# Two expert layers written in their own order, with the gate of a convolution layer and parts of an attention layer spread over other work

## The chip, the cores and the metric

The kernel runs on one core of one Trainium2 chip. The metric is the device time of one execution in microseconds (us), as the median of several runs. One further execution was recorded by the hardware profiler; durations of single instructions come from it.

A core has five engines that run at the same time, each through its own list of instructions in order: TensorE (PE in the profile) for matrix products, which writes to PSUM; VectorE (DVE), ScalarE (ACT) and GpSimd (POOL) for elementwise work; and SyncE (SP), which here only issues transfers (DMAs). PSUM has eight banks of 512 float32 columns on 128 partitions. An instruction that needs another engine's result waits on a semaphore, and everything behind it on its engine waits too.

## The reference

The input is `x` of shape (4, 128, 64, 64): four images of 128 channels and 4096 pixels. Four layers follow, all in float32.

```python
x = x + conv0(group_norm(x))                  # layer 0: deformable convolution
x = g * x + x                                 # layer 1, with
#   o = batch_norm(mamba_branch(x)); g = sigmoid(conv4_w^T o + conv4_b)
t = tokens(x)                                 # (4, 4096, 128)
t = t + attn2(layer_norm(t))                  # layer 2: cosines, products, a 2048-wide FFN of 8 inputs
t = t + moe2(layer_norm(t))                   #          eight experts, two used
t = t + attn3(layer_norm(t))                  # layer 3: additive tanh attention, causal
t = t + moe3(layer_norm(t))                   #          eight experts, two used
out = t back as (4, 128, 64, 64)
```

An expert layer computes, for each token `v` (128 values after the layer norm):

```python
p = softmax(v @ router_w + router_b)                  # 8 experts
top_p, top_i = top_k(p, 2); top_p = top_p / sum(top_p)
y = sum(top_p[k] * (v @ expert_w[top_i[k]] + expert_b[top_i[k]]) for k in 0, 1)
```

Attention of layer 3 is `w = tril(exp(w2 . tanh(f_i + g_j + b1) + b2))`, rows divided by their sums, times `v`.

## The kernel before, in words

The whole activation stays in SBUF as `X`, 128 partitions by 16384 columns. Through layers 0 and 1 partitions are channels; after that `X` holds tokens on partitions, as 128 tiles `T[:, t, :]` of 128 tokens by 128 channels. The stages run one after the other: layer 0, layer 1, the gate of layer 1, layer 2's attention and FFN, the first expert layer, attention of layer 3, the second expert layer, and a last transpose to channels (`flip`).

Where a stage uses `InOrder`, its instructions stand on each engine in the order in which the Python code writes them (they carry the line number 82 in the profile). Elsewhere a scheduler puts them in an order of its own, by what it expects to be ready.

**The gate (end of `layer1`).** The branch's output `o` lies in DRAM as 32 pieces `kept[k]` of 128 by 512. For each piece: a DMA reads it (`oin`), PE multiplies by `conv4_w` (`psg`), ACT takes the sigmoid (`g`), DVE computes `X = (g + 1) * X`. Two pieces later PE turns the piece's four 128 by 128 blocks to tokens (`psf`), and ACT (even pieces) or DVE (odd pieces) copies them back into `X`. All of it comes before layer 2.

**Layer 2 (`layer2`).** Sixteen groups of eight token tiles go through `slot(p, s)`: 17 + 3 passes `p` from -3 on, eight slots each. In a pass the FFN of group `p` runs on PE (`phh` hidden products, `pff` output products, 1024 of the latter in all), while group `p + 3` gets its moments and norm (`stA`, `u`, `c`), group `p + 2` its cosines and running products (`a`) and second norm, group `p - 1` its last norm and sum. The passes -3 to -1 prepare the first groups and have no FFN: a ramp.

**An expert layer (`moe`).** It is not in written order. It loads router and expert matrices on ACT's DMA queue, subtracts their last row from all others (so that the constant 1 in the last channel of `v` can carry the bias), and works in eight groups of 16 tiles. `route(g)`: moments on DVE (`bn_stats`), norm on ACT (`v`), 16 transposes on PE and copies on ACT (`vT`), 16 products of 8 columns for the logits with tokens on partitions (`psl`), then softmax and the two best experts in some 28 small DVE operations (`gate`). `experts(...)`: per tile two products of 512 columns (`pex`, 128 tokens by 8 experts by 128 channels, three buffers of two banks), one DVE multiplication by the gates over all 1024 columns (`x`), and then the sum over experts: for three tiles of four as three halving additions on POOL and a fourth that adds to `T`, for the fourth tile as one DVE reduction (`y`) and one POOL addition. `route(g + 1)` is written ahead of `experts(g)`.

**Attention (`attention`).** In written order, in 544 steps: 17 per block of 512 queries on average, `4 * ib + 3` for block `ib`. A step has products for a denominator (`D`) and, one step later, a numerator (`num`) on PE, logarithm and exponential on ACT (`r`), multiplications by `num` on DVE, two additions on POOL, and later the weighing (`acc`). `prepare` of the next block is cut into 8 parts (statistics, norm `v`, transposes and copy `vT`, four maps `F`, `G`, an end), spread evenly over a block's steps. After a block's last step `settle` transposes the sums, copies them (`zs`), divides and adds four tiles to `T`, all within one step. `D` has four banks; a step takes three of them, from bank 0 or 1 on (`side`). A part or a `settle` that needs bank 3 makes the step `taken`:

```python
taken = held[-1] is not None or any(p in ON_BANK for p in parts)
side = int(last[0] == 0 and not taken and not last[1])
again = side == last[0]
```

Where `again` holds, the same banks are used as in the step before, and PE begins with the numerator's products in place of the denominator's. The stage ends with a branch on a flag that all engines read.

**`flip`.** 32 rounds after the second expert layer: four transposes on PE (`psf`), a copy by DVE or ACT (`o`), a DMA of 256 KB to the output.

Of the kernel before, what the change touches and what calls it, by code (L numbers as in the profile page):

```python
# [88 lines left out]
class Kernel:  # L89
# [819 lines left out]
    def layer1(self):  # L909
# [9 lines left out]
        GS = NT // NG  # L919
        with ExitStack() as ctx:  # L920
# [4 lines left out]
            dram = ctx.enter_context(tc.tile_pool(name="l1d", bufs=1, space=DRAM))  # L925
# [8 lines left out]
            conv4_w = self.load(cp, "conv4_w", [P, P])  # L934
# [472 lines left out]
            sb = sp.tile([P, 1], F32, name="sb")  # L1407
# [9 lines left out]
            nc = InOrder(tc)  # L1417

            def gate(k):
                ks = slice(k * 512, (k + 1) * 512)  # L1420
                o = gp.tile([P, 512], F32, name="oin", tag="tm", bufs=4)
                plain.sync.dma_start(o, kept[k])
                ps = mm("psg")
                nc.tensor.matmul(ps, conv4_w, o, start=True, stop=True)
                g = gp.tile([P, 512], F32, name="g", tag="yT")
                nc.scalar.activation(g, ps, AF.Sigmoid, bias=sb)
                nc.vector.scalar_tensor_tensor(X[:, ks], g, 1.0, X[:, ks], ALU.add, ALU.mult)

            def to_tokens(k):
                ps = mm("psf")  # L1430
                for v in range(4):
                    c = k * 512 + v * P
                    nc.tensor.transpose(ps[:, v * P:(v + 1) * P], X[:, c:c + P], self.ident)
                dst = X[:, k * 512:(k + 1) * 512]
                if k % 2:
                    nc.vector.tensor_copy(dst, ps)
                else:
                    nc.scalar.copy(dst, ps)

            for k in range(NB * NG + 2):  # L1440
                if k < NB * NG:
                    gate(k)
                if k >= 2:
                    to_tokens(k - 2)

    def flip(self):

        tc, nc, X = self.tc, self.nc, self.X
        with ExitStack() as ctx:
            sp = ctx.enter_context(tc.tile_pool(name="flip", bufs=3))  # L1450
            pp = ctx.enter_context(tc.tile_pool(name="flipp", bufs=4, space=PSUM))
            for k in range(NB * 8):
                ps = pp.tile([P, 512], F32, name="psf")
                for v in range(4):
                    c = k * 512 + v * P
                    nc.tensor.transpose(ps[:, v * P:(v + 1) * P], X[:, c:c + P], self.ident)  # L1456
                o = sp.tile([P, 512], F32, name="o")
                if k % 2:
                    nc.vector.tensor_copy(o, ps)  # L1459
                else:  # L1460
                    nc.scalar.copy(o, ps)  # L1461
                nc.sync.dma_start(self.out[k // 8][:, (k % 8) * 512:(k % 8 + 1) * 512], o)
# [50 lines left out]
    def layer2(self):  # L1513
# [8 lines left out]
        with ExitStack() as ctx:  # L1522
# [25 lines left out]
            nc = InOrder(tc)  # L1548
# [5 lines left out]
            def stream(g):  # L1554
                return T[:, g * GT:(g + 1) * GT, :]

# [170 lines left out]

            ON_VECTOR = ((0, 1, 3), (1,), (1,), (1, 3), (1,), (1,), (1, 3), (1,))
# [52 lines left out]

            for p in range(-3, NG + 1):
                for s in range(8):
                    slot(p, s)

    def moe(self, layer):


        tc, nc = self.tc, self.nc
        GT = 16
        T = self.X.rearrange("p (t c) -> p t c", c=P)
        LAST = P - 1
        with ExitStack() as ctx:
            cp = ctx.enter_context(tc.tile_pool(name=f"m{layer}c", bufs=1))
            sm = ctx.enter_context(tc.tile_pool(name=f"m{layer}s", bufs=2))
            vp = ctx.enter_context(tc.tile_pool(name=f"m{layer}v", bufs=2))
# [4 lines left out]

            rw = self.load(cp, f"router_w{layer}", [P, NE])
            ew = self.load(cp, f"expert_w{layer}", [P, NE * P])
            last = cp.tile([P, P], F32, name="last")
            nc.vector.tensor_copy(last, self.ident[:, LAST:P].to_broadcast([P, P]))
            ps = pe.tile([P, NE, P], F32, name="psl_", tag="pex")
            psf = ps.rearrange("p e c -> p (e c)")
            for h in range(2):  # L1810
                nc.tensor.matmul(psf[:, 512 * h:512 * (h + 1)], last, ew[:, 512 * h:512 * (h + 1)],  # L1811
                                 start=True, stop=True)
            nc.vector.tensor_sub(ew, ew, psf)
            ps = pe.tile([P, NE, P], F32, name="psr_", tag="pex")
            nc.tensor.matmul(ps[:, 0, 0:NE], last, rw, start=True, stop=True)
            nc.vector.tensor_sub(rw, rw, ps[:, 0, 0:NE])
            nc.scalar.dma_start(ew[LAST:P, :], self.ins[f"expert_b{layer}"].rearrange("e c -> (e c)").unsqueeze(0))
            nc.scalar.dma_start(rw[LAST:P, :], self.ins["rows"][ROW[f"router_b{layer}"]].unsqueeze(0))
            vs = [cp.tile([P, GT, P], F32, name=f"v{i}") for i in range(2)]
            for v in vs:  # L1820
                nc.gpsimd.memset(v[:, :, LAST:P], 1.0)

# [5 lines left out]
            sh = [P, GT, NE]  # L1828

            def across(x):  # L1830
                return x.unsqueeze(2).to_broadcast(sh)

            def route(g):
                t = T[:, g * GT:(g + 1) * GT, :]
                v = vs[g % 2]
                mean, rstd = self.ln_stats(sm, t, GT)
                nmr = sm.tile([P, GT], F32, name="nmr")
                nc.vector.scalar_tensor_tensor(nmr, mean, -1.0, rstd, ALU.mult, ALU.mult)
                for k in range(GT):
                    nc.scalar.activation(v[:, k, 0:LAST], t[:, k, 0:LAST], AF.Identity,  # L1840
                                         bias=nmr[:, k:k + 1], scale=rstd[:, k:k + 1])
                vT = vp.tile([P, GT, P], F32, name="vT")
                for h in range(GT // 4):
                    ps = pv.tile([P, 512], F32, name="psv")
                    for k in range(4):
                        nc.tensor.transpose(ps[:, k * P:(k + 1) * P], v[:, 4 * h + k, :], self.ident)  # L1846
                    nc.scalar.copy(vT[:, 4 * h:4 * h + 4, :].rearrange("p t c -> p (t c)"), ps)
                psl = pl.tile(sh, F32, name="psl")
                for k in range(GT):
                    nc.tensor.matmul(psl[:, k, :], vT[:, k, :], rw, start=True, stop=True)  # L1850

                pr = sm.tile(sh, F32, name="pr")
                m = sm.tile([P, GT], F32, name="m")
                nc.vector.tensor_reduce(m, psl, AX.X, ALU.max)
                nc.vector.tensor_tensor(pr, psl, across(m), ALU.subtract)
                nc.scalar.activation(pr, pr, AF.Exp)
                nc.vector.tensor_reduce(m, pr, AX.X, ALU.add)
                nc.vector.reciprocal(m, m)
                nc.vector.tensor_tensor(pr, pr, across(m), ALU.mult)

                gate = sm.tile(sh, F32, name="gate")
                one = sm.tile(sh, F32, name="one")
                mx = sm.tile([P, 2, GT], F32, name="mx")
                rk = sm.tile([P, GT], F32, name="rk")
                for k in range(2):
                    nc.vector.tensor_reduce(mx[:, k, :], pr, AX.X, ALU.max)
                    nc.vector.tensor_tensor(one, pr, across(mx[:, k, :]), ALU.is_equal)
                    nc.vector.tensor_tensor(one, one, rank.unsqueeze(1).to_broadcast(sh), ALU.mult)
                    nc.vector.tensor_reduce(rk, one, AX.X, ALU.max)
                    nc.vector.tensor_tensor(one, one, across(rk), ALU.is_equal)  # L1870
                    if k == 0:
                        nc.vector.scalar_tensor_tensor(pr, one, -2.0, pr, ALU.mult, ALU.add)
                        nc.vector.tensor_tensor(gate, one, across(mx[:, 0, :]), ALU.mult)
                    else:
                        nc.vector.tensor_tensor(one, one, across(mx[:, 1, :]), ALU.mult)
                        nc.vector.tensor_add(gate, gate, one)
                nc.vector.tensor_add(m, mx[:, 0, :], mx[:, 1, :])
                nc.vector.reciprocal(m, m)
                nc.vector.tensor_tensor(gate, gate, across(m), ALU.mult)
                return g, vT, gate  # L1880

            def experts(g, vT, gate):
                for k in range(GT):
                    tk = T[:, g * GT + k, :]
# [4 lines left out]
                    x = xp.tile([P, NE, P], F32, name="x", bufs=4)  # L1889
                    nc.vector.tensor_tensor(x, pex, gate[:, k, :].unsqueeze(2).to_broadcast([P, NE, P]), ALU.mult)  # L1890
                    if k % 4 == 3:
                        y = xp.tile([P, P], F32, name="y")
                        nc.vector.tensor_reduce(y, x.rearrange("p e c -> p c e"), AX.X, ALU.add)  # L1893
                        nc.gpsimd.tensor_tensor(tk, tk, y, ALU.add)  # L1894
# [6 lines left out]
            for g in range(1, NB * NT // GT):  # L1901
                ahead = route(g)
                experts(*held)
                held = ahead
            experts(*held)

# [588 lines left out]
```

## Time and profile before

| | us |
|---|---|
| median of 3 runs | 5567.05 (5563.71 to 5577.1) |
| the profiled execution's own time | 5584.88 |
| its span, first to last instruction | 5583.2 |
| gate of layer 1 | about 1938 to 1985 |
| ramp of layer 2, until PE is full | about 1985 to 2049 |
| layer 2, PE full | 2049 to 2691 |
| first expert layer: start, first `x`, end | 2710, 2746.7, about 3058 |
| attention | about 3055 to 5201 |
| second expert layer: start, first `x`, last POOL addition | 5207, 5241.5, 5554.5 |
| last output transfer issued | 5579 |

Stages are read off the first and last start of the tiles named above. In the profile a group is one kind of instruction; "busy" is the time in which the engine ran it, "mean" the duration of one, and the part behind the bar is the time in which the engine stood idle just before, with the engine and tile that ended it. A float32 product of 512 columns shows as two records.

### The profile page before, as it was taken

What the parts mean: (1) busy time and instruction counts of PE and PEld (TensorE: products, weight loads), DVE (VectorE), ACT (ScalarE), POOL (GpSimd) and SP (SyncE); (2) the same over time, 40 slices, a digit from 0 to 9 for tenths busy, and PEclk for the clock granted to TensorE, in tenths of its full rate; (3) what the DMA queues carried; (4) which work ended last, traced back from release to release, by engine and by line L of the source; (5) the groups of instructions that cost most, each with busy time, mean ns of one, the idle gap of its engine ahead of it and who ended that gap; (6) DMA issues with size and microseconds to landing.
All of it is one profiled execution on the core that took longest, in us unless ns stands there. A gap on an engine that the chain in (4) does not pass through costs nothing. (4 is left out here: it accounts for less than half of the span.)

```text
span 5583.2 us, 62833 instructions
## 1 busy us (share of the span) xinstructions
PE 4990.0 (89%) x21718; PEld 2405.5 (43%) x21718; DVE 4020.2 (72%) x7854; ACT 3113.5 (56%) x3785; POOL 3102.9 (56%) x3027
## 2 busy tenths in 40 slices
PE   5898999879999859999887899989998998999887
PEld 3454444436666523333443344434443444444443
DVE  6888898758875577886697665666566666665796
ACT  1221222146654445555421789878988997889431
POOL 0625355414443334543498567666766776667597
PEclk8999999989988779999899899999999999999899
DMA  5545455300000110000000000000000000000001
GB/s 173 133 124 127 127 143 129 83 6 5 12 16 16 41 44 1 1 1 1 6 31 31 1 1 1 1 1 1 1 1 1 1 1 1 1 1 1 5 1 61
DMA packets 66743, 185.21 MB, mean 33 GB/s; under 512 B 13158, under 2 KB 16038, under 8 KB 64744
## 3 DMA queue, kind: packets, MB, share of 16 engines
q1 hardware_dynamic: 55792, 163.68, 9.9%
q0 software_dynamic: 6272, 12.86, 1.4%
q10 hardware_dynamic: 4344, 4.50, 0.3%
q8 instruction: 175, 2.87, 0.2%
q14 instruction: 160, 1.31, 0.1%
HBM read 131.63 MB, written 49.36 MB: 32 GB/s over the span
## 5 line engine op out<-in xcount | busy, mean ns | idle before, releaser
L82 POOL TENSOR_TENSOR r<-r 128x512 f32<-128x512 f32 (+1 forms) x1088 | 1348.7, 1241 | 666.1 <-DVE r L82 610.3
L82 DVE TENSOR_TENSOR r<-r,num 128x1024 f32<-128x1024 f32 (+1 forms) x1088 | 969.9, 926 | 565.0 <-PE num L82 518.1
L82 PE MATMUL D<-F,G 32*128 32x512 f32 (+3 forms) x4608 | 1223.1, 591 | 1.9 <-POOL G L82 1.0
L82 PE MATMUL num<-F,G 32*128 32x512 f32 (+3 forms) x4608 | 1090.1, 606 | 105.0 <-DVE r L82 101.0
L82 ACT ACTIVATE r<-r 128x2048 f32<-128x2048 f32 (+4 forms) x610 | 1018.4, 1679 | 49.2 <-POOL r L82 3.4
L82 ACT ACTIVATE r<-D 128x1536 f32<-128x1536 f32 (+1 forms) x544 | 764.2, 1405 | 210.4 <-PE D L82 178.2
L82 PE MATMUL acc<-pr,ident 128*128 128x512 f32 x1600 | 736.2, 609 | 63.2 <-DVE pr L82 63.0
L82 PEld LDWEIGHTS D<-F,G 32*128 32x128 f32 x4608 | 505.3, 190 | 326.0 <-issue 216.3
L82 PE MATMUL acc<-r,v 128*128 128x512 f32 (+3 forms) x1152 | 608.1, 615 | 2.9 <-DVE aT L82 2.9
L82 PEld LDWEIGHTS num<-F,G 32*128 32x128 f32 x4608 | 394.8, 187 | 414.0 <-DVE r L82 236.1
L1887 PE MATMUL pex<-w_expert_w,vT 128*128 128x512 f32 x1024 | 490.8, 619 | 77.6 <-DVE x L1890 77.5
L1897 POOL TENSOR_TENSOR x<-x 128x512 f32<-128x512 f32 (+2 forms) x576 | 472.3, 820 | 103.5 <-DVE x L1890 73.4
L82 POOL DMA_INDIRECT px<-tab,idx x196 | 359.4, 1834 | 295.1 <-DVE idx L82 158.5
L82 PEld LDWEIGHTS acc<-pr,ident 128*128 128x128 f32 x1600 | 303.7, 195 | 414.1 <-issue 330.3
L82 DVE TENSOR_TENSOR pr<-v,wt 128x2560 f32<-128x2560 f32 x160 | 453.9, 2843 | 30.7 <-PE acc L82 23.6
L82 PE MATMUL pff<-hid,w_ffn_w2T 128*128 128x512 f32 x1024 | 468.9, 601 | 0.0
L1890 DVE TENSOR_TENSOR x<-pex,gate 128x1024 f32<-128x1024 f32 x256 | 309.0, 1213 | 61.5 <-POOL X L1898 49.9
L82 PEld LDWEIGHTS acc<-r,v 128*128 128x128 f32 x1152 | 177.6, 191 | 395.8 <-issue 266.3
L1887 PEld LDWEIGHTS pex<-w_expert_w,vT 128*128 128x128 f32 x1024 | 184.8, 194 | 328.0 <-DVE x L1890 174.2
L82 ACT ACTIVATE hid<-phh,cols 128x512 f32<-128x512 f32 x320 | 198.9, 685 | 224.7 <-PE phh L82 224.7
L82 POOL TENSOR_TENSOR Y<-y,tm 128x64 f32<-128x64 f32 x256 | 115.4, 471 | 331.9 <-DVE w L82 159.9
L82 POOL TENSOR_TENSOR X<-X,sl 128x512 f32<-128x512 f32 x32 | 90.1, 2817 | 376.1 <-ACT sl L82 376.1
(563 smaller groups left out, 7390.4 us busy)
## 6 DMA issues: line engine op xcount, KB each, us to landing
v<-tab SPq DMA_DIRECT2D x320, 256.0 KB, 3.9
oms<-omw SPq DMA_DIRECT2D x32, 432.0 KB, 3.3
omr<-oms SPq DMA_DIRECT2D x32, 432.0 KB, 4.4
X<-in_x_dram SPq DMA_DIRECT2D x8, 1024.0 KB, 10.6
tab<-vb SPq DMA_DIRECT2D x64, 128.0 KB, 2.7
o<-o SPq DMA_DIRECT2D x32, 256.0 KB, 2.0
oin<-o SPq DMA_DIRECT2D x32, 256.0 KB, 2.8
kept<-X SPq DMA_DIRECT2D x4, 2048.0 KB, 6.3
```

Of the source, the lines that this page charges most:

```text
L82: return lambda *args, **kwargs: self.tc.keep_in_program_order(op(*args, **kwargs))
L1887: nc.tensor.matmul(pex[:, 4 * h:4 * h + 4, :], vT[:, k, :], ew[:, 512 * h:512 * (h + 1)], start=True, stop=True)
L1890: nc.vector.tensor_tensor(x, pex, gate[:, k, :].unsqueeze(2).to_broadcast([P, NE, P]), ALU.mult)
L1897: nc.gpsimd.tensor_tensor(x[:, 0:w, :], x[:, 0:w, :], x[:, w:2 * w, :], ALU.add)
```

## The change

**Gate.** Its code moves out of `layer1` into `layer2`, and is called as `gate(k)` from the ramp: four pieces ahead of pass -3, eleven in each of passes -3 and -2 (`GATES`), eight in pass -1 (`LAST_GATES`). All copies of turned pieces are on ACT. The pieces `oin` now live in a pool of layer 2, and their DMAs stand on SP's queue behind the loads of layer 2's FFN matrices and of the first expert layer's matrices.

**Expert layers.** `moe_load` loads matrices early on SP's queue: those of layer 2 ahead of layer 2, those of layer 3 ahead of the first expert layer. `moe_prepare` does the subtraction of the last row and lays the router out as four 128 by 128 matrices `rws`, each with its 8 columns at a place of its own. `moe` is in written order: nine groups of 8, 8, 16, ... tiles; `experts(i, s)` handles a pair of tiles per slot, and the steps of `gates` (group `p + 1`), `logits` (`p + 2`) and `moments` (`p + 3`) are dealt out over the slots. Logits are now four products of 512 columns per group into one bank, with experts on partitions, copied by ACT (`lT`) and turned by four transposes. Of the eight experts ACT weighs three of each tile (`x[:, u, 0:3]`). In even slots DVE weighs the other five one by one, four of them adding to a partial sum already there, so that POOL has 4 planes left to add; in odd slots DVE multiplies the five at once and POOL adds 8 planes. POOL's additions take both tiles of a pair. The square root of the norm is replaced by `exp(-0.5 * ln(...))`.

**Turning out.** In the second expert layer `flip(q)` is called after every second pair, two quads behind, with copies on ACT; the last two follow the loop.

**Attention.** `statistics` has three pauses in place of none, `settle` is cut into `settle`, `ratio` and `onto`, which take one step each, and the parts of `prepare` are dealt out from a block's first step on, one per step while there are fewer parts than steps, in place of evenly.

```diff
+            GATES, LAST_GATES = (0, 1, 1, 1, 2, 2, 2, 2), (0, 1, 1, 1, 2, 2, 1, 0)
...
+            for _ in range(4):
+                gate(next(steps))
             for p in range(-3, NG + 1):
                 for s in range(8):
                     slot(p, s)
+                    for _ in range(GATES[s] if p < -1 else LAST_GATES[s] if p < 0 else 0):
+                        gate(next(steps))
...
+                    for e in range(3):
+                        nc.scalar.activation(x[:, u, e, :], pex[:, e, :], AF.Identity, scale=gate[:, k, e:e + 1])
+                    if at_once:
+                        nc.vector.tensor_scalar(x[:, u, 3, :], pex[:, 3, :], gate[:, k, 3:4], None, ALU.mult)
+                        for e in range(4):
+                            nc.vector.scalar_tensor_tensor(x[:, u, e, :], pex[:, 4 + e, :],
+                                                           gate[:, k, 4 + e:5 + e], x[:, u, e, :],
+                                                           ALU.mult, ALU.add)
                     else:
...
+                        nc.vector.tensor_tensor(x[:, u, 3:NE, :], pex[:, 3:NE, :],
+                                                gate[:, k, 3:NE].unsqueeze(2).to_broadcast([P, 5, P]), ALU.mult)
+                for w in (2, 1) if at_once else (4, 2, 1):
+                    nc.gpsimd.tensor_tensor(x[:, :, 0:w, :], x[:, :, 0:w, :], x[:, :, w:2 * w, :], ALU.add)
+                nc.gpsimd.tensor_tensor(T[:, t0:t0 + 2, :], T[:, t0:t0 + 2, :], x[:, :, 0, :], ALU.add)
...
+                def product(h):
+                    nc.tensor.matmul(psl, rws[:, h, :], vT[:, 4 * h:4 * h + 4, :].rearrange("p t c -> p (t c)"),
+                                     start=h == 0, stop=h == n // 4 - 1)
...
+                        if layer == 3 and pairs % 2 == 0 and pairs >= 6:
+                            flip(pairs // 2 - 3)
...
-                later = [lambda *a: a, weigh, settle]
+                later = [lambda *a: a, weigh, settle, ratio, onto]
...
-                    taken = held[-1] is not None or any(p in ON_BANK for p in parts)
+                    taken = held[SETTLES] is not None or any(1 <= p <= 5 for p in parts)
...
-                        to = -(-PARTS * max(r - first + 1, 0) // (rounds - first))
-                        step((n, ib, parts, r == rounds - 1), range(done, max(done, to)))
-                        done = max(done, to)
+                        now = ()
+                        if ahead is not None and r >= first:
+                            now = range(done, done - (done - PARTS) // (rounds - r))
+                            done = now.stop
+                        step((n, ib, parts, r == rounds - 1), now)
...
+    with ExitStack() as gate:
+        k.layer1(gate)
+        k.moe_load(two, 2)
+        k.layer2()
     k.attention_maps(ctx)
-    k.moe(2)
+    k.moe_load(ctx, 3)
+    with two:
+        k.moe_prepare(two, 2)
+        k.moe(2)
     k.attention()
+    k.moe_prepare(ctx, 3)
     k.moe(3)
-    k.flip()
```

## The prediction

> **What bounds the kernel now.** I read the page's busy shares first, then busy time by stage, then in each stage the groups by form and the waits.
>
> ```profile
> span 5583.2 us, 62833 instructions
> PE 4990.0 (89%) x21718; PEld 2405.5 (43%) x21718; DVE 4020.2 (72%) x7854; ACT 3113.5 (56%) x3785; POOL 3102.9 (56%) x3027
> ```
>
> PE is full for 89%, so 593 us of PE idleness are the whole stake. By stage (length, then busy us of PE, PEld, DVE, ACT, POOL):
>
> ```profile
> 1938.00:1985.00 47.00, 44.92 (x192) 25.59 (x192) 33.12 (x53) 31.83 (x51) 2.35 (x3) 0.94 0.59 175
> 1985.00:2049.00 64.00, 8.02 (x24) 3.01 (x25) 46.53 (x136) 16.53 (x23) 27.75 (x25) 0.52 0.01 5
> 2049.00:2691.00 642.00, 641.08 (x2277) 254.92 (x2276) 469.48 (x1260) 364.80 (x629) 278.16 (x211) 1.00 0.00 1
> 2710.00:2747.00 37.00, 26.13 (x118) 18.57 (x118) 27.68 (x154) 25.35 (x60) 0.38 (x4) 0.68 0.05 15
> 2747.00:3055.00 308.00, 263.13 (x784) 122.44 (x784) 276.73 (x386) 63.99 (x131) 284.86 (x409) 0.98 0.05 21
> 3090.00:5195.00 2105.00, 1960.18 (x10827) 855.50 (x10826) 1320.71 (x2039) 1814.98 (x1302) 1442.68 (x1150) 0.97 0.00 1
> 5546.00:5583.00 37.00, 21.12 (x128) 16.32 (x128) 14.15 (x19) 9.37 (x16) 8.27 (x13) 0.85 0.59 227
> ```
>
> The reader is to see: the gate is PE's and the ramp nobody's (DVE 73%, PE 13%), so they can overlap; layer 2 is PE's; the first expert layer is POOL's (285 of 308), DVE close, ACT nearly free; attention has 145 us of PE idleness; the flip stands alone. Groups in the expert layer, the form behind the names, then count, busy, mean ns:
>
> ```profile
> L1887 PE MATMUL pex<-w_expert_w,vT 128*128 128x512 f32 x455 | 216.1, 616 | 33.0 <-DVE x L1890 32.9
> L1890 DVE TENSOR_TENSOR x<-pex,gate 128x1024 f32<-128x1024 f32 x114 | 137.8, 1212 | 18.5 <-POOL X L1898 12.8 <-PE pex L1887 5.1 <-POOL X L1894 0.5
> L1897 POOL TENSOR_TENSOR x<-x 128x512 f32<-128x512 f32 x84 | 107.0, 1274 | 37.5 <-DVE x L1890 37.5
> L1897 POOL TENSOR_TENSOR x<-x 128x256 f32<-128x256 f32 x84 | 61.4, 731 | 6.6
> ```
>
> **Part 1, the gate inside the ramp: -14.** Gate and ramp take 1938 to 2048 = 110. What goes: 47 us of gate alone, and 16 DVE copies (.68 each, 11 us). What comes to the ramp: PE 32 x 1.3 = 42 (8 busy of 64 now); ACT 32 x (.69 sigmoid + .58 copy) = 41 on 17; DVE 32 products x .69 = 22 on 46.5 = 68.5, so DVE bounds it. The transfers: on SP's queue `oin` now stands behind the FFN matrices (1 MB, issued after `mv` ends at 1934.7, landing takes 5.0), the store of the last `o` and four issues of .75; the first `oin` lands at about 1943 by its row of 2.8, the third waits for the MB. First gate product 5.5 late. The ramp's DVE leaves 17.5 idle now (64 less 46.5, waits along the chain of norms and cosines), which I keep: 68.5 + 17.5 + 3.5 for table loads, from 1944 on, puts the first FFN products at 2034 in place of 2048. Table loads on ACT, as sigmoid now alternates with the ramp's sine and square root, grow from 7 to 12. Here a rule speaks against the change: the Trainium skill, "ScalarE: Activation LUTs", "What ACT_TABLE_LOAD costs", charges about 2.66 us per switch, load plus drain. The trace shows 1.31 from the end of one activation (1997.83) to the start of the next (1999.14). I take the row: 5 x 1.3 = 6.5, in the 14; by the rule 13, and the gain is 7. ACT (58 + 6.5 of 90) hides half of it; if sigmoids wait behind turned pieces all through, the part is +5; if the gate's work fills those 17.5 and hides the loads, the part is -28 or a little more.
>
> Layer 2's full part keeps its instructions and order: 0, covered by PE at 641 of 642.
>
> **Part 2, first expert layer: -25.** Start: the matrices are there already, but two small bias DMAs still come behind the subtraction, and `rws` copies stand on DVE ahead of the moments. A group of 8 in place of 16 is normed first: first `x` at about 2739 in old time, not 2746.7: -8. Then per pair of tiles:
> - before: POOL (3 x (1.27 + .73 + .46 + .46) + .46) / 2 = 4.6; the measured pace is 4.87.
> - PE after: products 8 x .427 = 3.41, transposes .30, a 512 product per four tiles .43, turns .08: 4.2.
> - DVE after: the row of 1.212 for 1024 columns is .146 + 1024/960. Even slots: ten operations of 128 columns at .27, 2.7; odd slots two of 640 columns at .81, 1.63; mean 2.15; gates (28 small ones per group, 8.3) 1.04, moments .75: 3.94.
> - POOL after: even 1.35 + .80 + .80 = 2.95, odd 2.35 + .08 + 2.94 = 5.37; mean 4.15 (its three rows lie on .185 + 2.12 ns a column, so 1024 columns take 2.35; one instruction per pair saves a start).
> - ACT after: six weighings, two norms of .385, copies .45. No row shows this weighing (PSUM in, one pointer). From below, the page above: 186 + 93 for the pointer + 107 for the columns less 93 of overlap = .29; from above the norm with two pointers, .385 (fast form) to .48. I take .34: 3.3 in all, up to 4.1.
>
> Three engines within 7% of 4.2. Before, pace over bound was 1.06; with three near-equal engines in fixed order I take 1.09: 4.6. Sixty-four pairs x .27 = 17 gained, with the start 25. In the loop PE, ACT, DVE a `pex` buffer is held 1.7 + 1.0 + 1.3 plus hand-overs, about 4.5, and three buffers at 2.3 per tile allow 6.9: that cover hides ACT's lateness of up to 2.4. Behind DVE's wait for ACT stand the gates' steps; behind PE's wait for DVE (PSUM of `psv` and `psg` is one buffer) stand products; I put 1 to 1.5 per group, in the 1.09. Range of the part: -50 (pace 4.3) to +10.
>
> The second weighed rule: DVE additions of two SBUF operands.
>
> ```profile
> L1867 DVE TENSOR_TENSOR one<-pr,mx x2: 270/272/273, 5235.7 to 5238.0; 128x128 f32<-128x128 f32 x2
> ...
> L1875 DVE TENSOR_TENSOR one<-one,mx x7: 276/629/1229, 5263.2 to 5499.3; 128x128 f32<-128x128 f32 x7
> ```
>
> First row: POOL idle; second: POOL busy, the longest as long as one POOL addition of 512 columns. "SBUF — State Buffer", "SBUF: two separate sides", says such a DVE operation and a GpSimd one exclude each other for the whole instruction. POOL's longest rises from 1.27 to 2.35, so by the rule gates pay 5.7 per group in place of 3.6: +.27 per pair, DVE 4.2. By the rows alone (an old mean of .6) 3.94. The weighing reads one operand from PSUM and isn't touched. I take the rule for the 1.09, and its size for the slow rival.
>
> **Part 3, attention: -35.**
>
> ```profile
> PE num L82 <- DVE r L82: 101.0, 96, 2.9
> ```
>
> That is 101 of PE's 145 idle us, in 96 waits: PE stands before `num` because DVE is late. By the gaps' places, about 45 are at a `settle`, 17 at statistics, 50 at `v`. `settle` puts 3.3 us of DVE work into a step in which DVE has 1.9 to spare (3.9 less 1.8 of multiplying and less the rest), statistics 2.7; cut into three steps each fits. So settle and statistics mostly go (-62 x .75 = -46), `v` is not cut and stays. `again` steps, counted by the rule in the code, fall from 241 to 180 of some 550. Against it: two more steps to drain (about 5), and parts that come one per step from a block's start meet `settle`, `ratio` and `onto` there (36 meetings, .15 each): +11. From -65 to +10.
>
> **Part 4, second expert layer with the flip inside: -26.** Start only 3 earlier (a cold start, nothing hides it). PE per pair gets .30 of turning: 4.5, x 1.09 = 4.9, 64 pairs = 314, against 313 before. ACT gets .29 per pair and stays below 4. The 37 us of flip go, and 8 come back: the last POOL addition (5.4), two turned quads, a DMA of 2. 3 - 1 + 29 less 5 for blocks out of turn = 26. Output DMAs, 256 KB per 10 us, lie beside it; uncovered they cost a transfer each, 2 x 32, which nothing in their issue order asks for. From -60 to +15.
>
> **Sum.** -14 - 25 - 35 - 26 = -100: span 5583 to 5483. The profiled execution (5584.88) is .3% above the median of the runs, so the median goes from 5567 to 5468.
>
> **The rivals.**
> - *Written order eats the expert gain.* Pairs at 4.87 (5.2 with flips), as before: three engines alternate where the scheduler filled. For: in odd slots POOL (5.4) is over the pace, in even ones (2.95) below; the fixed order can let both show. Against: three `x` buffers even it out. Costs +17 and +20: 5505.
> - *Attention gives nothing.* Parts dealt out early meet the cut `settle`, waits move rather than go: 5503; with the one above 5540.
> - *All engines overlap better.* Pairs 4.3 and 4.6, attention -70, gate -25: about 5381.
> - *Slower: the even slots' chain.* A tile's five DVE operations wait for its three ACT ones, those for PE's last product, POOL for DVE, while gates stand on DVE behind a 2.35 us POOL addition. If the chain cannot overlap across tiles, a tile costs its chain of about 3 rather than 2.3: pairs 5.9 and 6.2, +164 in both layers: 5631. It decides from .78 per pair on (+100). For: ACT is new in the chain and its list also holds norms. Against: the buffer account above, with 2.4 to spare.
> - That the change does not do what it says is excluded by the order of instructions: sigmoids stand between the ramp's steps, flips between pairs.
>
> **How the numbers follow.** My forecast .50 (own range 5430 to 5505); order eats the gain .21; attention nothing, alone or with it, .09; better .07; slow chain .13. Low 5405 and high 5545 leave out the slow chain and most of the better case. No measurement of this kernel can tell .3% (17 us) from no change: faster .85, same .02 (out of attention nothing, with pairs slower yet), slower .13.
>
> **What would show it.** First gate product at 1943 and FFN products from 2034; first `x` of the first expert layer 8 earlier against its stage's start; pairs 4.6 and 4.9; waits of `num` on DVE down from 101 to about 65; the last output transfer about 8 after the last POOL addition. Wrong: weighing on ACT over .45; DVE waiting for ACT by over 1 per pair; PE waits before `num` unchanged; FFN products later than 2048.

## The result, and the profile after

The changed kernel takes 5598.99 us (median of 6 runs, 5587.43 to 5613.43), the kernel before 5567.81 beside it: ratio 1.005, 95% interval 1.003 to 1.0071. Recorded again later it was 5600.62 against 5579.21, ratio 1.0043 (1.0028 to 1.0058). It is slower by 21 to 31 us; the forecast was 100 faster.

The page of the changed kernel, in the form shown of before:

```profile
span 5585.7 us, 63127 instructions
PE 5007.2 (90%) x21406; PEld 2369.3 (42%) x21406; DVE 4091.4 (73%) x8304; ACT 3333.0 (60%) x4608; POOL 3030.3 (54%) x2643
```

Each engine's share looks as before, and the page alone would call the change neutral. Busy time by stage (length, then PE, PEld, DVE, ACT, POOL, granted clock): gate and ramp; layer 2 full; start of the first expert layer; its loop; attention; loop of the second; tail.

```profile
1913.00:2016.60 103.60, 63.20 (x219) 33.53 (x220) 71.10 (x180) 64.83 (x97) 35.51 (x28) 0.81 0.32 96
2016.60:2657.30 640.70, 639.65 (x2277) 254.31 (x2276) 469.61 (x1260) 364.75 (x628) 278.21 (x211) 1.00 0.00 1
2670.00:2705.70 35.70, 23.40 (x49) 11.26 (x49) 15.85 (x88) 15.71 (x37) 6.59 (x6) 0.58 0.06 15
2705.70:3075.00 369.30, 299.69 (x718) 128.46 (x716) 310.90 (x716) 179.47 (x555) 250.60 (x233) 0.91 0.06 23
3095.00:5178.00 2083.00, 1955.20 (x10833) 845.33 (x10825) 1383.08 (x2042) 1809.93 (x1301) 1443.53 (x1150) 0.98 0.00 1
5221.00:5568.00 347.00, 296.20 (x825) 135.50 (x823) 303.97 (x690) 190.08 (x576) 240.19 (x216) 0.95 0.06 23
5568.00:5585.70 17.70, 2.12 (x9) 0.98 (x8) 0.82 (x1) 2.24 (x6) 8.94 (x9) 0.58 0.12 45
```

POOL did less work than before (251 in place of 285 in the first loop), as meant, and the loop is longer all the same, because DVE is busy for 311 in place of 277. The granted clock in this loop is lower too (.91, before .98), but a product took 626 ns in place of 616, which is 5 us over the loop's 512 records, so the clock is not the loss. The stages, from starts and ends in the two traces (the first `x` is VectorE's first):

| stage | before | after | difference | predicted |
|---|---|---|---|---|
| last batch-norm moment to first FFN product | 114.4 | 102.7 | -11.7 | -14 |
| FFN products | 642.5 | 641.3 | -1.2 | 0 |
| to first `x` | 55.1 | 47.8 | -7.3 | -8 |
| first `x` to first `num` | 344.3 | 388.2 | +43.9 | -17 |
| first `num` to last `zs` | 2106.8 | 2083.8 | -23.0 | -35 |
| to first `x` of the second expert layer | 43.8 | 42.9 | -0.9 | -3 |
| first `x` to last POOL addition | 313.5 | 356.8 | +43.3 | +1 |
| to the end | 28.2 | 8.3 | -19.9 | -29 and +5 for its blocks out of turn |

They sum to +23, which agrees with the medians. Of the 123 us between forecast and sum, 103 lie in the two expert loops. The spans differ by only 2.5, because in this one execution layers 0 and 1, whose code did not change, ended 21 us earlier at a higher granted clock. The last 400 us of layer 1, before and then after:

```profile
1530.00:1934.00 404.00, 373.65 (x1948) 243.36 (x1947) 255.71 (x844) 197.29 (x374) 162.44 (x262) 0.82 0.05 18
```

```profile
1530.00:1913.00 383.00, 348.88 (x1942) 227.52 (x1940) 252.53 (x838) 196.81 (x374) 163.05 (x261) 0.88 0.05 18
```

The same work of PE took 349 in place of 374 at .88 in place of .82, so that stage is no part of the change.

The loss lies in the two expert loops. Groups of the first, between 2710 and 3045 (count, busy us, mean ns, idle before):

```profile
L82 PE MATMUL pex<-w_expert_w,vT 128*128 128x512 f32 x499 | 240.6, 626 | 34.0 <-DVE x L82 30.3 <-ACT x L82 3.2
L82 ACT ACTIVATE x<-pex,gate 128x128 f32<-128x128 f32 x372 | 107.1, 367 | 98.4 <-PE pex L82 66.4 <-DVE mean L82 12.3 <-DVE gate L82 7.1
...
L82 POOL TENSOR_TENSOR x<-x 128x1024 f32<-128x1024 f32 x30 | 70.4, 2347 | 56.9 <-DVE x L82 44.2 <-DVE m L82 12.5
L82 DVE SCALAR_TENSOR_TENSOR x<-pex,gate,x 128x128 f32<-128x128 f32 x244 | 67.9, 338 | 0.0
L82 DVE TENSOR_TENSOR x<-pex,gate 128x640 f32<-128x640 f32 x62 | 49.0, 815 | 21.4 <-ACT x L82 19.8 <-issue 1.1 <-POOL x L82 0.4
...
L82 DVE TENSOR_TENSOR one<-one,rk 128x128 f32<-128x128 f32 x14 | 24.5, 1748 | 0.5
L82 DVE TENSOR_TENSOR one<-pr,mx 128x128 f32<-128x128 f32 x14 | 23.5, 1679 | 0.5
...
L82 DVE TENSOR_TENSOR gate<-one,mx 128x128 f32<-128x128 f32 x7 | 15.0, 2147 | 0.0
```

The new operations cost no more than was estimated: the weighing on ACT .367 from start to end, with the next starting .25 after it (estimate .34 in a row), five experts at once .815 (.81), POOL's 1024 columns 2.347 (2.35), the single weighing on DVE .338 from start to end, with the next starting .26 after it (.27). The last three rows are the surprise: gate steps with two operands in SBUF and 128 columns, .27 where POOL is idle, take 1.7 to 2.1 us on average. Their waits stand in no row of waits; the trace counts them as busy. The order of time shows what they are:

```profile
2864.75 0.28 DVE L82 TENSOR_REDUCE mx<-pr 128x16 f32<-128x128 f32 x1
2864.91 4.48 POOL L82 TENSOR_TENSOR x<-x 128x1024 f32<-128x1024 f32 x3 [1.93 <-DVE x L82]
2865.06 2.35 DVE L82 TENSOR_TENSOR one<-pr,mx 128x128 f32<-128x128 f32 x1
2867.45 1.30 DVE L82 TENSOR_TENSOR one<-one,rank 128x128 f32<-128x128 f32 x1
...
2870.57 2.53 PE L82 MATMUL pex<-w_expert_w,vT 128*128 128x512 f32 x3 [2.61 <-DVE x L82]
```

POOL's first addition runs from 2864.91 to 2867.26, and the DVE step that began beside it ends at 2867.41; the next step waits out the next addition. Of the 97 gate operations with two SBUF operands from 2700 on in this stage, 74 took over .6 us, and each of these ended .08 or .15 us after the end of a POOL instruction. While DVE waits no `x` is made; PE runs out of buffers (2.61 idle before the last line), and then POOL stands waiting for DVE:

```profile
POOL x L82 <- DVE x L82: 106.5, 47, 31.4
```

One of these waits, 31.4, is the start of the stage; the others, 1.6 on average, are the answer. Before, POOL waited for `x` once in this loop, at its start:

```profile
POOL x L1897 <- DVE x L1890: 37.5, 1, 37.5
```

In the changed kernel POOL holds DVE up, and is then held up by DVE: two engines that should run side by side take turns.

### The profile page after: what moved, and what is told of

The parts are those of the page before. It is cut to its first block, busy times and chain, and to the rows that moved or that the text cites. A ratio compares the mean times of both kernels' runs of the same rounds, so it can differ in the third digit from the quotient of the medians.

```text
span 5585.7 us, 63127 instructions
## 1 busy us (share of the span) xinstructions
PE 5007.2 (90%) x21406; PEld 2369.3 (42%) x21406; DVE 4091.4 (73%) x8304; ACT 3333.0 (60%) x4608; POOL 3030.3 (54%) x2643
## 5 line engine op out<-in xcount | busy, mean ns | idle before, releaser
L82 PE MATMUL D<-F,G 32*128 32x512 f32 (+3 forms) x4608 | 1235.8, 586 | 1.0 <-POOL G L82 1.0
L82 PE MATMUL num<-F,G 32*128 32x512 f32 (+3 forms) x4608 | 1075.2, 600 | 79.6 <-DVE r L82 78.2
L82 POOL TENSOR_TENSOR x<-x 128x512 f32<-128x512 f32 (+2 forms) x320 | 406.2, 1269 | 259.1 <-DVE x L82 185.3
L82 ACT ACTIVATE x<-pex,gate 128x128 f32<-128x128 f32 x768 | 221.1, 366 | 195.9 <-PE pex L82 132.4
L82 PEld LDWEIGHTS pex<-w_expert_w,vT 128*128 128x128 f32 x1024 | 196.1, 201 | 292.1 <-issue 216.4
```

The costliest lines, as they stand in the source:

```text
L82: return lambda *args, **kwargs: self.tc.keep_in_program_order(op(*args, **kwargs))
```

## The experiments

Theory L: these waits, of DVE's two-operand steps on POOL's additions, are the loss. Theory C, the rival: the fixed order and the new chain PE, ACT, DVE, POOL set the pace. Pace is the mean time per pair of tiles from VectorE's first to its last `x`; in the kernel before it is 4.8.

**The old expert layers and flip, with the new gate and attention.**

```diff
-    k.moe_load(two, 2)
...
-    k.moe_prepare(ctx, 3)
     k.moe(3)
+    k.flip()
```

> The moved gate and the changed attention stay; both expert layers and the final flip are those of the kernel before. Theory L (in the new expert layers VectorE's gate steps, which read two SBUF operands, wait out GpSimd's additions, and GpSimd then waits for VectorE): all of the loss lies in the expert layers, so this kernel keeps the gain of the other parts, about 12 us at gate and ramp and 23 in attention: 5567 - 35 = 5533. Theory C (the fixed order and the new chain PE, ACT, DVE, POOL set the pace) expects the same here. A third reading, that gate or attention gained only by a better clock in the one profile, expects 5555 to 5567.

Measured 5543.34 against 5576.22: ratio .9937 (.9922 to .9953), 33 us less. From the batch norm to the first FFN product it took 103.2 (114.4 before), and attention 2094.0 (2106.8). So gate and attention do gain (attention 13 here, 23 in the changed kernel's trace), and the whole loss sits in the expert layers.

**Four two-operand gate steps in place of twelve.**

```diff
-                nc.vector.tensor_reduce(m, pr, AX.X, ALU.add)
-                nc.vector.reciprocal(m, m)
-                nc.vector.tensor_tensor(pr, pr, across(m), ALU.mult)
...
+                nc.vector.scalar_tensor_tensor(one, pr, 1.0, pr, ALU.is_lt, ALU.mult)
+                nc.vector.tensor_reduce(mx, one, AX.X, ALU.max)
+                nc.vector.tensor_scalar(m, mx, 1.0, None, ALU.add)
+                nc.vector.reciprocal(m, m)
+                nc.vector.tensor_tensor(one, pr, across(mx), ALU.is_ge)
+                nc.vector.tensor_tensor(gate, one, pr, ALU.mult)
+                nc.vector.tensor_tensor(gate, gate, across(m), ALU.mult)
```

The largest probability, before division, is exactly 1, and the sum cancels. Equal probabilities are not ranked any more.

> The changed kernel, with the gates worked out in four VectorE operations of two SBUF operands per group in place of twelve (no division by the softmax's sum, which cancels, and no ranking of ties). L: two thirds of some 12 us of waiting per group go, and the eight operations' own 2.2 us, together 10 per group or 1.2 us per pair; VectorE falls from 4.8 to 3.6 busy per pair and PE or GpSimd sets a pace of 4.6 in place of 5.4: 50 us less in each expert layer, about 5500. C: VectorE's gate steps are not what the chain waits for; pace 5.2, at most 15 us less per layer, about 5570.

Measured 5522.82: ratio .9903 (.9889 to .9918), about three quarters of the gain that L expected. The first loop's pace is 4.62 per pair, as L has it; the second's is 5.01, which it has not. The gate steps, in the groups from 2710 to 3000:

```profile
L82 DVE TENSOR_TENSOR gate<-gate,m 128x128 f32<-128x128 f32 x7 | 3.8, 546 | 0.0
L82 DVE TENSOR_TENSOR gate<-one,pr 128x128 f32<-128x128 f32 x7 | 3.0, 436 | 0.0
```

All such steps in that stretch together take 13.9 us, where in the changed kernel they take 122.6 (2710 to 3045). That is more than two thirds less: with fewer of them not only the number but each one's wait is smaller.

**Shorter additions.**

```diff
-                for w in (2, 1) if at_once else (4, 2, 1):
-                    nc.gpsimd.tensor_tensor(x[:, :, 0:w, :], x[:, :, 0:w, :], x[:, :, w:2 * w, :], ALU.add)
+                for u in range(2):
+                    for w in (2, 1) if at_once else (4, 2, 1):
+                        nc.gpsimd.tensor_tensor(x[:, u, 0:w, :], x[:, u, 0:w, :], x[:, u, w:2 * w, :], ALU.add)
```

> The changed kernel, with GpSimd's additions per tile in place of per pair: the longest takes 1.27 us in place of 2.35, at .4 to .65 us more GpSimd work per pair. L: the locked gate steps fall from a mean of 1.3 us to .8, some 5 us per group, .6 per pair, of which the longer GpSimd work eats a part: pace 5.0, 5600 - 45 = 5555. C: GpSimd's part of the chain grows, nothing else changes: pace 5.4 to 5.8, 5600 to 5640.

Measured 5564.35: ratio .9979 (.997 to .9988), 35 to 40 us under the changed kernel though POOL has more work. Paces 5.00 (as L has it) and 5.20. Two of the steps that were shown of the changed kernel, from 2710 to 3030:

```profile
L82 DVE TENSOR_TENSOR one<-pr,mx 128x128 f32<-128x128 f32 x14 | 8.4, 603 | 0.5
L82 DVE TENSOR_TENSOR one<-one,rk 128x128 f32<-128x128 f32 x14 | 8.2, 583 | 0.5
```

No gate step was touched, and these two are about a third as long (all of them .56 on average): their length is that of what they wait for.

**No halving additions.**

```diff
-                for w in (2, 1) if at_once else (4, 2, 1):
-                    nc.gpsimd.tensor_tensor(x[:, :, 0:w, :], x[:, :, 0:w, :], x[:, :, w:2 * w, :], ALU.add)
```

> The changed kernel without GpSimd's halving additions: only plane 0 of x is added to the tokens, the sum over the other planes is left out. VectorE keeps all its instructions. L: GpSimd is busy .7 us per pair, gate steps run at .27 to .4 us, VectorE falls to 3.4 per pair and PE sets the pace, 4.3 to 4.5 (4.6 to 4.8 with the turning): about 5480. C: the part PE, ACT, DVE of the chain is all there, and the fixed order too: pace 5.2 or more, 5570.

This kernel leaves out the sum over the other planes. Measured once: 5477.72. Paces 4.45 and 4.88. The groups from 2710 to 3000, all twelve steps still there:

```profile
L82 DVE TENSOR_TENSOR one<-one,rank 128x128 f32<-128x128 f32 x14 | 4.1, 292 | 0.5
L82 DVE TENSOR_TENSOR one<-pr,mx 128x128 f32<-128x128 f32 x14 | 4.1, 292 | 0.5
```

None takes .3. The order, ACT's place in the chain and DVE's list are all unchanged. Taken alone, this run takes away POOL's share of the chain too; but the four-step kernel has all of POOL's additions and the whole chain, and its first loop is at 4.62. The two together leave theory C no room for the 44 us.

**The turning ahead of the pair.** On top of the four-step gates:

```diff
+                        if layer == 3 and pairs % 2 == 0 and pairs >= 4:
+                            flip(pairs // 2 - 2)
                         experts(p, s)
                         pairs += 1
-                        if layer == 3 and pairs % 2 == 0 and pairs >= 6:
-                            flip(pairs // 2 - 3)
```

It was aimed at these waits of PE in the second expert loop of the kernel with four-step gates (5190 to 5500):

```profile
PEld psv L82 <- ACT o L82: 23.5, 12, 3.4
...
PE psv L82 <- ACT o L82: 16.3, 11, 3.2
```

> The changed kernel with the four-operation gates, and in the second expert layer each turned quad is written ahead of its slot's pair in place of behind it. In the kernel with the four-operation gates alone PE waits some 40 us in that layer for ScalarE's copy of a turned quad, because the copy stands behind six weighings that wait for PE. If those waits are what makes the second layer slower than the first (5.0 against 4.6 per pair), the pace falls to 4.6 to 4.7 and the time by 20 us, to about 5500 on a chip where the kernel before takes 5570. If it is PE's own turning (.3 per pair), nothing changes: 5520.

A miss: 5541.91, ratio .9932 (.9911 to .9952). The waits of PE on the copy fell from 40 us to 1.4, but the second loop's pace is 5.20 in place of 5.01; DVE waits for ACT's weighing for 90 us there, in place of 74, behind the copy. The spans of the two kernels differ by 26: 9 of it lies in this loop, 24 in layers 0 and 1, whose instructions are the same, and -7 in the rest. So the total by itself says little of the edit; the stage says that it did not help.

**Two experts on ACT.** On top of that, a plane moves from ACT to DVE:

```diff
-                    for e in range(3):
+                    for e in range(2):
                         nc.scalar.activation(x[:, u, e, :], pex[:, e, :], AF.Identity, scale=gate[:, k, e:e + 1])
...
-                        nc.vector.tensor_scalar(x[:, u, 3, :], pex[:, 3, :], gate[:, k, 3:4], None, ALU.mult)
+                        for e in (2, 3):
+                            nc.vector.tensor_scalar(x[:, u, e, :], pex[:, e, :], gate[:, k, e:e + 1], None, ALU.mult)
```

> As the kernel with four-operation gates and the turning written first, and ScalarE weighs two experts of each tile in place of three; VectorE takes the third (+.4 us per pair), ScalarE has .7 less. Theory C's part that is left: VectorE waits 66 us per layer for ScalarE's weighings; if that chain sets the rest of the pace (4.6 against PE's 4.3 busy), it falls to 4.45, 10 us less in each layer, about 5480. If PE alone is the bound by now, no change, 5500.

5538.57, ratio .993 (.9908 to .9952); paces 4.66 and 5.16 against 4.67 and 5.20. No change: the chain by way of ACT does not set what is left.

**The parts of attention dealt out evenly; the settling in one step.** Two variants of the changed kernel, each measured once:

```diff
-                            now = range(done, done - (done - PARTS) // (rounds - r))
+                            now = range(done, low - (low - PARTS) * (r - first + 1) // (rounds - first))
```

```diff
-                later = [lambda *a: a, weigh, settle, ratio, onto]
+                later = [lambda *a: a, weigh, lambda *a: onto(*ratio(*settle(*a)))]
```

> The changed kernel with the parts of the attention's preparation dealt out evenly over a block's steps, as before; the divided settling and statistics stay. Read by the attention stage alone, 2084 to 2094 us from the first numerator product to the last copy of the sums, 2107 before. If parts that come early meet the settling there, as the prediction charged (+11), the stage is 2075 to 2085. If the early dealing is itself the gain, it is 2095 to 2107. Total near 5600.

> The changed kernel with the settling, the ratio and the adding in one step again, so two steps fewer to drain; the rest as changed. The prediction's step was that the settling in one step leaves PE waiting some 45 us, of which three quarters would go: then the stage is 2115 to 2125 here, longer than before. If the cut of the settling gives nothing, it stays at 2084 to 2094. Total near 5600 to 5630.

Both are misses, above all that was expected of them: 5651.02 and 5664.22 in all, and the stage took 2126.0 with even parts and 2140.7 with the whole settling. The granted clock differs between these stages (.97 and .95, .98 in the changed kernel), so I compare PE's idle time, length less busy: before 145.7, changed 127.5, even parts 150.2, whole settling 147.3. All eleven recordings with the changed attention lie between 127 and 132, so these differences are no scatter. Each half of the change alone gains nothing; the two together gain 18. PE's waits in the changed kernel, and with even parts:

```profile
PE num L82 <- DVE r L82: 78.2, 100, 1.8
```

```profile
PE num L82 <- DVE r L82: 87.4, 103, 1.9
PE D L82 <- DVE v L82: 28.9, 10, 6.6
```

Dealt out late, `v` makes PE wait 29 us for the next block; dealt out early, 10 (its row in the changed kernel has 9.7). The even dealing changes something else as well: by the rule for `again`, 248 steps use the same banks twice in a row, in the changed kernel 180 and before 241. No run separates the two.

**The gate steps in a bunch.** All twelve are kept, but in one slot:

```diff
+                        due = -(-a[1] * (s + 1) // slots)
+                        if a[1] == 9 and a is beside[0] and p + 1 < N:
+                            due = (0, 1, 9)[min(s, 2)]
-                        while a[2] < -(-a[1] * (s + 1) // slots):
+                        while a[2] < due:
```

> The changed kernel, with the same twelve two-operand gate operations per group, but all steps of a group's gates written in one slot, behind its exponential one slot earlier, in place of one or two steps in every slot. L: in a bunch the first two or three operations wait out GpSimd's queue; then no new x has come, GpSimd stands, and the rest run at .27. Waiting falls from 12 us per group towards the 3.5 of the kernel before, where the scheduler had them close together; but the bunch itself (8 us, and the wait) stops the experts once per group. Pace 4.9 to 5.1, some 45 us less than the changed kernel in all. C: same instructions, more burst: 5.4 or more, no gain.

Half a miss: 5610.67, ratio 1.0048 (1.0031 to 1.0064), no faster than the changed kernel, where L expected 45 us less. The waits went as L says (2710 to 3045):

```profile
L82 DVE TENSOR_TENSOR one<-pr,mx 128x128 f32<-128x128 f32 x14 | 5.1, 366 | 0.5
L82 DVE TENSOR_TENSOR one<-one,rk 128x128 f32<-128x128 f32 x14 | 4.2, 303 | 0.5
```

All 108 gate steps of the layer take 41 us in place of 125, and 82 of them began with POOL idle, but the pace is 5.45. The time from one pair's first product on PE to the next, over the eight slots of one full group, shows why:

| kernel | slots of one group, us | sum |
|---|---|---|
| changed | 7.2, 6.4, 3.4, 9.3, 5.5, 3.4, 4.7, 4.3 | 44.2 |
| bunched | 3.7, 7.6, 3.4, 4.7, 11.8, 3.4, 4.7, 4.3 | 43.6 |
| shorter additions | 5.8, 5.7, 3.4, 4.9, 6.7, 3.4, 4.7, 4.3 | 38.9 |
| four steps | 3.9, 5.4, 3.4, 4.7, 5.5, 3.4, 4.7, 4.3 | 35.3 |
| no additions | 3.9, 4.7, 3.4, 4.7, 5.5, 3.4, 4.7, 4.3 | 34.6 |

The bunch costs 9 us (11.8 where others have 5.5, and 7.6 for 4.7). It keeps DVE for 6.6 us; meanwhile PE fills the free `pex` buffers and then stands 4.2 us for DVE's `x`, and shortly before it stood 2.0 us for DVE's `pr`. So "less waiting" is not itself the remedy. Steps that are dealt out cost next to nothing while POOL leaves them alone (last row), and steps in a bunch cost their own length. By PE's instructions a group takes about 34.

**The changed and the four-step kernel once more,** on one chip with the bunched one:

> The changed kernel once more, to have it beside the others on one chip. Both theories: 1.005 of the kernel before, expert pace 5.4, GpSimd-locked gate operations 122 us per layer. Open is where layers 0 and 1 end: 1914 us in the first profile, 1935 in the kernel before, with the same instructions; if that is a state of the clock and not of the kernel, it may be either here.

> The kernel with four-operation gates once more, beside the changed one: 76 us less than that (0.986), paces 4.6 and 5.0; .990 of the kernel before.

5600.62 and 5518.08, ratios 1.0043 (1.0028 to 1.0058) and .9888 (.987 to .9905): 83 us between them. Paces 5.38 and 5.49 against 4.67 and 5.06. Layers 0 and 1 ended at 1918 and 1917, close to the first recordings of these two (1914 and 1915).

**Eight groups of sixteen,** with the four-step gates:

```diff
-        SIZES = [8, 8] + [16] * 7
+        SIZES = [16] * 8
```

> The four-operation gates, and eight groups of 16 tiles in place of 8, 8 and seven of 16. In the kernel with four-operation gates a full group takes 35 us in eight slots, near PE's own 34, but the first eight slots, which belong to the groups of 8 and carry the norms and logits of groups of 16 behind them in half the slots, take 57. What is left of theory C (the fixed order makes ScalarE's norms late) sits there. With equal groups the first x comes about 8 us later (the start before took 55 against 47), and the first eight slots take 36 to 40: 10 to 14 us less in each layer, .985 of the kernel before, about 5495 where that takes 5579. If the filling of the buffers and not the group size makes the first slots slow, only the later start stays: 15 us more, .9915.

5519.92, ratio .9881 (.9865 to .9897), no different from the four-step kernel. Both of the expected parts are in the trace: the first eight slots fall from 57 to 36 us and the paces to 4.32 and 4.68, but the first `x` comes 64.4 after the FFN, not 55. What the small groups lose in the loop they gain, for the most part, at the start.

## Why the prediction was wrong

One term of the sum turned a gain into a loss: what a gate step waits for POOL. The rest was off by much less.

- *Pace of the expert loops* (4.6 and 4.9 per pair): 5.40 and 5.48. This step failed. Its bound for PE was right (4.2; without the additions a group takes 34.6 us, 4.3 per pair), those for POOL and ACT were high (4.15 and 3.3; busy 3.8 and 2.8 between 2710 and 3045), and so was DVE's own work: busy 4.8 per pair, less 1.6 of waiting 3.2, where the prediction had 3.94 with .45 of waiting. What failed is the term "by the rule gates pay 5.7 per group in place of 3.6": the waits came to 12 per group (122.6 us per layer, less 96 steps of .27, over eight groups). The Trainium skill, "SBUF — State Buffer", "SBUF: two separate sides", was stated rightly (whichever starts first holds the port "for the whole instruction") and agrees with the ends of the 74 steps above. But what such a lock costs depends on where in POOL's addition a step begins, and that was not carried through. I scaled the old mean of about .6:

```profile
L1867 DVE TENSOR_TENSOR one<-pr,mx 128x128 f32<-128x128 f32 x14 | 7.8, 557 | 0.0
```

```profile
2913.51 2.60 POOL L1897 TENSOR_TENSOR x<-x 128x512 f32<-128x512 f32 x3
2914.32 0.61 DVE L1867 TENSOR_TENSOR one<-pr,mx 128x128 f32<-128x128 f32 x1
```

  That mean belongs to a POOL that is the slowest engine and works through `x` that lies ready, so that a step meets its additions part way, here .8 us after the start of a 1.27 us one. (The steps did not stand in a bunch there, as I had supposed for the bunched kernel: before most of them stands an `x`.) Of the 84 steps of the first loop before, 78 began in a POOL instruction, half of them more than .33 us after its start, and it ran on for .43 on average. The changed POOL has less work and waits for DVE's `x`; it starts when that is done, and so does DVE's next instruction, a gate step. Of 96 steps 82 began in a POOL instruction, 64 of them within .2 us of its start, and it ran on for 1.31 on average. (This is counted in the two traces; no run moved the starts alone.) So a step takes 1.28 on average, up to 2.47. And with 4.8 of busy time per pair DVE is itself the slowest engine, so no buffer hides its waits. The 1.09 for "near-equal engines" had room for .4 per pair, not for 1.
- *The signs of being wrong* that were named did not come: the weighing on ACT took .37, DVE waited for ACT .45 per pair, PE's waits before `num` fell, and the FFN products came at 2017. None of the four watches how long a gate step takes.
- *The slow rival* had the place and the point of decision right ("gates stand on DVE behind a 2.35 us POOL addition", from .78 per pair on): +.80 and +.58 came. Its other half, a chain that can't overlap across tiles, is refuted by the four-step kernel, which keeps the chain and takes 4.62, and its price (5.9 and 6.2) was too high. It was given 13%, because I set the buffers' slack against it; that slack counts for ACT's lateness and not for a lock between DVE and POOL.
- *Gate in the ramp* (-14): -11.7, over all kernels with it between -11.0 and -14.0. The first gate product stood 9.0 after the batch norm's last moment, predicted 8.3. Table loads took 1.28 each.
- *Start of the first expert layer* (-8): -7.3.
- *Attention* (-35): -23 in this trace and -13 to -23 over the recordings of the same code; PE's idle time fell by 18. Waits before `num` fell from 101 to 78, not to 65. That the sum came near is luck, for two terms were wrong in opposite ways. The -46 for cutting settling and statistics did not come from the cut: with even parts both are cut, and PE's idle time is 150, not below 145.7. And the early dealing, charged with about 5 of the +11, is what makes the cut pay: without it the idle time is 23 larger. Besides, the additions of the cut settling, with two operands read from SBUF, took .343 before; after:

```profile
L82 DVE SCALAR_TENSOR_TENSOR X<-zs,den,X 128x127 f32<-128x127 f32 x128 | 82.5, 703 | 0.0
```

  With the whole settling they take .344. Cut, they run beside POOL's additions: the 51 of them over .45 us all ended .15 us after the end of a POOL instruction. It is the same lock. What these 46 us of DVE cost the stage is not shown; no run here takes POOL away in attention.
- *Turning inside* (-26 with its start): the stretch after the last POOL addition is 8.3, as predicted, but it was 28 before, so that 20 are saved and not 29. The prediction counted 37 us of `flip` from its first turned quad at 5546, while the 313 us of its loop run to the last addition at 5554.5: nine us stood in both. Put into the loop, the quads cost .1 per pair in the changed kernel, where DVE is the bound, and .4 where PE is (4.62 and 5.01 with four steps): 25 us, more than the 20 that the tail saves.

## What to carry to other kernels

Before spreading small VectorE steps of two SBUF operands over a loop, look at what GpSimd runs there and what starts it. Each step can last as long as a GpSimd instruction, and it does where both start on the same event. Shorten GpSimd's instructions or have fewer steps; fewer was best here, .989 of the kernel before where the change alone gave 1.004. Feeding one operand from PSUM may help too; no run tried it on these steps. And read a mean together with the state it was measured in: .6 us was the cost of a step beside a GpSimd that ran behind, and said little of the same step beside one that waits for VectorE.

## What the runs showed of the hardware

A VectorE step blocked in this way counts as busy and stands in no list of waits: it shows only as a mean of 1.7 us for a form that takes .27 elsewhere. VectorE's weighing, which reads one operand from PSUM, was not held up (.338 with the additions, .342 without them).

Layers 0 and 1 have the same instructions in all kernels. The granted clock between 1560 and 1900 us was .89 in six recordings and .85 to .87 in the eight others, and layer 1 ended at 1914 to 1923 or at 1931 to 1939 accordingly. The two kernels recorded twice fell in the first group both times. But a recorded execution of the first group took at most as long as its kernel's median (within .4 us), and one of the second at least as long, wherever there were several; so the difference seems to lie in the execution and not in the kernel. What decides it stays open; it is 20 us, as much as the effects that were looked for.
